# Eigenvector products at other places in TensorE's order, and a plain third weight for the last two groups of layer 0

## The chip, the cores and the metric

The kernel runs on one core of a Trainium2 chip. The metric is the time on the device in microseconds (us), from the start of the program to its end. Three runs of the kernel before took 2317.26, 2320.21 and 2320.10 us, so the median is 2320.1 us.

## What is computed

Four layers run one after the other over x of 128 x 64 x 256 values. Each adds what its branch gives to x and normalises the rows. Only layers 0 and 1 matter here:

```python
# layer 0: three graph convolutions, the adjacency multiplied twice (adj * S with S = adj)
h = relu(slconv(x, adj, adj, W1)); h = relu(slconv(h, adj, adj, W2)); slconv(h, adj, adj, W3)
x = layernorm(x + ...)
# layer 1: the eigenvectors of the normalised Laplacian of adj
L_norm = d_inv_sqrt[:, None] * (diag(deg) - A) * d_inv_sqrt[None, :]
_, U = eigh(L_norm)                       # 64 x 64
agg = einsum('mn,bnd->bmd', U.T, x); h = relu(agg @ W1 + b1)
x = layernorm(x + einsum('nm,bmd->bnd', U, h @ W2 + b2))
# layer 2: two graph convolutions and LSTMs over windows of 1 to 4 steps; layer 3: attention
```

U depends on `adj` alone. So it can be computed while layer 0 runs, and layer 1 is the first that needs it.

## The kernel before

The 8192 rows lie in 64 tiles of 128 rows, and four tiles make a group. **Layer 0** (function `layer0`, L1116) goes through 16 groups, the twelve groups 4 to 15 of the rows first and then 0 to 3 (`order`, L886). In this text a group is called by its place in that loop, so the last two are 14 and 15. **Layers 1 to 3** follow for all groups, in an order that a planner (`Plan`) writes out; the two phases share no work but a few row norms.

One group of layer 0 on TensorE is, in this order:

- the second weight (L1131): for each of two halves j, seven products of blocks instead of eight (`seven`, L1056), each of four calls of 128 x 256 columns. VectorE adds sums of blocks ahead of them (`sums_second`, L1109) and adds partial products together after them; ScalarE copies and applies relu. The result is `h2`, the 1024 features of 512 rows.
- after the first half, the adjacency product (`burst`) of the next group.
- the third weight (L1138): seven products again (`by_third`), each of eight calls of 128 columns. VectorE makes `sh[:, 0]`, `sh[:, 1]` and two differences in `h2` for them (L1141, L1142, L1147, L1148), each over 1024 elements per partition, and adds three results into `s3`. Between the second and the third of these products stand the four products of the next group's first weight (`weigh`).
- two more bursts of the next group, and `mix_rows`, which multiplies `s3` by the adjacency. VectorE then adds that into X.

In group 15 there is no next group, so `weigh` and the bursts are missing.

**The eigenvectors** (function `eigen`, L275) run beside this. They are a chain of small steps on VectorE: 62 Householder steps with one product on TensorE each (L415), two small products and two row broadcasts, six passes of bisection with 31 division steps each (L563), 63 further division steps (L603 to L608, tiles `tw` and `D`), and a tail with nine more products on TensorE (L643 to L749). The last of them fill `u2` and `ut2`, which layer 1 multiplies by.

The order of each engine's instructions is fixed when the program is built. `mm` in layer 0 (L963) emits a product and moves a reckoned clock `now` on by its expected time; `between` (L953) then lets `eigen` emit its next piece as soon as `now` has reached the time that `eigen` yielded. Its yields are `soon()` (L306), 0.45 us ahead of the end of VectorE's reckoned work, and `full()` (L309), which stands ahead of a product on TensorE. `free` is that reckoned end: each VectorE instruction of layer 0 and of `eigen` moves it on (class `Timed`, L42). So the place of an eigenvector product in TensorE's order, and of each eigenvector instruction between layer 0's instructions on VectorE, follow from these two clocks. After layer 0 whatever is left of `eigen` is emitted at once (L1169), and layers 1 to 3 come after it in every queue.

Of the kernel before, what the change touches and what calls it, by code (L numbers as in the profile page):

```python
# [11 lines left out]
F32 = mybir.dt.float32  # L12
# [262 lines left out]
def eigen(tc, stack, a, ident, cst, u2, ut2, now, free):  # L275
# [10 lines left out]
    until = [0.0]  # L286
    V, S, PE = Timed(nc.vector, free, until), nc.scalar, nc.tensor
# [5 lines left out]
    def sb(shape, tag):  # L293
        uid[0] += 1
        return wp.tile(shape, F32, tag=tag, name=f"{tag}_{uid[0]}")
# [10 lines left out]
        return max(free[0], until[0]) - 0.45  # L306

    def full(turns=0):
        return max(free[0], until[0]) + 0.3 + 0.6 * turns  # L309

    def mm(out, lhsT, rhs):
        PE.matmul(out, lhsT, rhs, start=True, stop=True)  # L312
# [37 lines left out]
    V.tensor_scalar(dm, C["eye"], y, None, op0=ALU.mult)  # L350
    pm = ps([N, N], "pa")
    yield full(4)
    mm(pm, m, dm)

# [27 lines left out]
    for i in range(N - 2):  # L382
# [3 lines left out]
        q = sb([N, 16], "q")  # L386
# [67 lines left out]
    d, e, ep, g = (de[:, j:j + 1] for j in range(4))  # L454
# [101 lines left out]
    lo2, h2, lam2 = lh[:, 0:1], lh[:, 1:2], lh[:, 2:3]  # L556
# [46 lines left out]
    for k in range(1, N):  # L603
        c = N - 1 - k
        t = sb([W, 1], "tw")
# [149 lines left out]
P = 128  # L755
# [13 lines left out]

RING = 4  # L770
QUADS = 1.17


def norm_parts(tc, pool, x, half, scalar=False):
# [54 lines left out]
def kernel(  # L829
# [26 lines left out]
    V, S, PE = nc.vector, nc.scalar, nc.tensor  # L856
# [5 lines left out]
    def tl(pool, shape, tag, **kw):  # L862
        uid[0] += 1
        return pool.tile(shape, F32, tag=tag, name=f"{tag}_{uid[0]}", **kw)
# [6 lines left out]
    wa = phase_a.enter_context(tc.tile_pool(name="wa", bufs=1))  # L871
# [4 lines left out]
    def load(pool, name, src, pattern, shape, **kw):  # L876
        t = pool.tile(shape, F32, name=name)
        nc.sync.dma_start(t, src.rearrange(pattern, **kw))
        return t
# [8 lines left out]
    def rows_of(g):  # L888

        return X[:, 4 * g:4 * g + 4, :] if g < RING else XA[:, 4 * (g - RING):4 * (g - RING) + 4, :]  # L890
# [16 lines left out]
    aw3 = load(wa, "aw3", a_w3, "(k p) f -> p k f", [P, 8, D], p=P)  # L907
# [45 lines left out]
    def between():  # L953
        while eig and eig[0] <= now[0]:
            try:
                eig[0] = next(eig[1])
            except StopIteration:
                eig.clear()
        if norms and due[0] <= now[0]:
            norms.pop(0)()  # L960
            due[0] = now[0] + 1.6

    def mm(out, lhsT, rhs, start=True, stop=True, **kw):  # L963
        PE.matmul(out, lhsT, rhs, start=start, stop=stop, **kw)  # L964
        now[0] += 2 * max(0.00084 * rhs.free_size(), 0.112)
        between()

    def run(out, pairs):
        for i, (lhsT, rhs) in enumerate(pairs):
            mm(out, lhsT, rhs, i == 0, i == len(pairs) - 1)  # L970

    def relu(dst, src):
        S.activation(dst, src, AF.Relu)  # L973

    def quads(c):
        for m in (slice(0, N), slice(N, P)):
            for h, hs in enumerate((slice(0, N), slice(N, P))):
# [3 lines left out]
    B11, B12, B21, B22 = (aw2[:, r:r + 2, c:c + 512] for r in (0, 2) for c in (0, 512))  # L981
    tw = wa.tile([P, 3, 2, 512], F32, name="tw")
    D11, D12, D21, D22 = (aw3[:, r:r + 4, c:c + P] for r in (0, 4) for c in (0, P))
    tv = wa.tile([P, 3, 4, P], F32, name="tv")
    m1 = pa.tile([P, 2, 512], F32, name="m1")
    h1 = pa.tile([P, 4, 512], F32, name="h1")
    m2 = pa.tile([P, 4, 512], F32, name="m2")
# [1 line left out]
    h2 = pa.tile([P, 8, 512], F32, name="h2")  # L989
    sh = pa.tile([P, 2, 4, 256], F32, name="sh")  # L990
    s3 = pa.tile([P, 4, D], F32, name="s3")
    A11, A12, A21, A22 = (m2[:, k:k + 2, r:r + 256] for r in (0, 256) for k in (0, 2))
    H11, H12, H21, H22 = (h2[:, c:c + 4, r:r + 256] for r in (0, 256) for c in (0, 4))
# [1 line left out]

    second = ((None, B11, B21, B22, tw[:, 2], B12, tw[:, 1], tw[:, 0]),
              (None, A11, A12, ss[:, 2], A22, ss[:, 0], ss[:, 1], A21))
    third = ((None, D11, D21, D22, tv[:, 2], D12, tv[:, 1], tv[:, 0]),
             (None, H11, H12, H12, H22, sh[:, 0], sh[:, 1], H21))
    free = [0.0]  # L1000
    VL = Timed(V, free, now)
# [3 lines left out]
    def step(then=None):  # L1005

        while pending:
            pending.pop(0)()
        if then:
            pending.append(then)  # L1010
        if norms:
            norms.pop(0)()

    def bank(tag="ps"):
        return tl(psa, [P, 512], tag, bufs={"ps": 4, "ch": 2, "b5": 1}[tag])

    def sums_of_weights(w, b12):
        VL.tensor_sub(w[7], w[3], b12)
        VL.tensor_sub(w[5], b12, w[1])
        VL.tensor_sub(w[6], w[3], w[5])  # L1020
        VL.tensor_sub(w[4], w[2], w[6])

    def burst(dst, src, c):
        to = dst.rearrange("p c (t h n) -> p h c t n", h=2, n=N)
        p = [bank().rearrange("p (c t n) -> p c t n", c=2, t=4) for _ in range(2)]
        for t in range(4):
            for k in range(2):
                for m, f, h, hs in quads(c + k):
                    PE.matmul(p[h][m, k, t, :], src[hs, t, f], sqT2[hs, hs], start=True, stop=True)  # L1029
        now[0] += QUADS  # L1030
        between()

        def result():
            for h in range(2):
                S.copy(to[:, h, c:c + 2], p[h])  # L1035

        step(result)
# [6 lines left out]
    def by_second(j):  # L1044

        def product(out, i, new):
            w, a = (x[i] for x in second)
            chained(out, [[(w[:, k, c * P:(c + 1) * P], a[:, k, :]) for k in range(2)] for c in (2 * j, 2 * j + 1)], new)

        return product  # L1050
# [5 lines left out]
    def seven(n, product, c11, c12, c21, c22, last):  # L1056

        def view(b):
            return b[:, :2 * n].rearrange("p (i n) -> p i n", i=2)

        def add(dst, b):
            VL.tensor_add(dst, dst, b)
            if last is relu:
                relu(dst, dst)

        ch = view(bank("ch"))
        product(ch, 1, True)
        step(lambda: S.copy(c11, ch))
        yield
        b2 = view(bank())  # L1070
        product(b2, 2, True)
        step(lambda: add(c11, b2))
        yield
        product(ch, 6, False)
        step(lambda: S.copy(c12, ch))
        yield
        b5 = view(bank("b5"))
        product(b5, 5, True)
        step(lambda: S.copy(c22, b5))
        yield  # L1080
        product(ch, 7, False)
        step(lambda: add(c22, ch))
        yield
        product(b5, 3, False)
        step(lambda: add(c12, b5))
        yield
        product(ch, 4, False)
        step(lambda: last(c21, ch))
        yield

    def weigh(t):
        p = bank()
        run(p, [(m1[:, k, t * P:(t + 1) * P], aw1[:, k, :]) for k in range(2)])
        step(lambda: relu(h1[:, t, :], p))
# [14 lines left out]
    def sums_second():  # L1109
        S1, S2, S4 = (ss[:, i] for i in range(3))  # L1110
        VL.tensor_add(S1, A21, A22)
        VL.tensor_sub(S2, S1, A11)
        VL.tensor_sub(A21, A11, A21)
        VL.tensor_sub(S4, A12, S2)

    def layer0():  # L1116
        n = NT // 4
        burst(m1, rows_of(order[0]), 0)
        step()
        for t in range(4):  # L1120
            weigh(t)
        step()
        sums_of_weights(second[0], B12)
        for c in (0, 2):
            burst(m2, h1, c)
        step()
        for g in range(n):
            sums_second()
            for j in range(2):
                q = [h2[:, 4 * c + 2 * j:4 * c + 2 * j + 2, r:r + 256] for r in (0, 256) for c in (0, 1)]  # L1130
                for _ in seven(256, by_second(j), *q, relu):  # L1131
                    pass
                if j == 0 and g + 1 < n:
                    burst(m1, rows_of(order[g + 1]), 0)
                if j == g == 0:
                    sums_of_weights(third[0], D12)
            q = [s3[:, r:r + 2, c:c + P] for r in (0, 2) for c in (0, P)]
            w3 = seven(P, by_third, *q, S.copy)  # L1138
            next(w3)
            next(w3)  # L1140
            VL.tensor_add(sh[:, 0], H21, H22)  # L1141
            VL.tensor_sub(sh[:, 1], sh[:, 0], H11)  # L1142
            for t in range(4):
                if g + 1 < n:
                    weigh(t)
                if t == 0:
                    VL.tensor_sub(H21, H11, H21)  # L1147
                    VL.tensor_sub(H12, H12, sh[:, 1])  # L1148
            for _ in range(4):
                next(w3)  # L1150
            if g + 1 < n:
                burst(m2, h1, 0)
            next(w3)
            if g + 1 < n:
                burst(m2, h1, 2)
            for t in (0, 2):
                mix_rows(g, t)
        step()
# [71 lines left out]
    V, S, G, Q = (Noted(plan, e) for e in ("DVE", "ACT", "POOL", "SP"))  # L1230
# [62 lines left out]
    def mixed(src, rhs):  # L1293
# [4 lines left out]
        plan.note("PE", [("matmul", (ps[h][m, c, t, :], src[hs, t, f], rhs[hs, hs]), {"start": True, "stop": True})  # L1298
                         for t in range(4) for c in range(2) for m, f, h, hs in quads(c)], QUADS)
        V.tensor_copy(to[:, 0], ps[0])  # L1300
# [433 lines left out]
```

## Time and profile before

One execution was profiled: 2317.55 us, of which the profiled span is 2315.7 us. Its mean granted TensorE clock is 0.988 of full speed.

| Stretch of the span | What runs | TensorE busy | VectorE busy |
|---|---|---|---|
| 55 to 105 us | layer 0 with Householder steps | 50.00 of 50 us | 41.39 us |
| 554 to 826 us | layer 0 with bisection and the further steps | 267.38 of 272 us | 231.87 us |
| 826 to 846 us | the tail of `eigen` alone | 3.89 of 20 us | 15.93 us |
| 846 to 2316 us | layers 1 to 3 | 1432.51 of 1470 us | 1069.36 us |

In this and the other views busy time is that of instructions that run; what stands in brackets behind a line of a timeline is how long the engine sat idle before it, and what ended that. TensorE appears in two rows: PE is the products and PEld is their weight loads. One product call of 32-bit numbers appears as two records. DVE is VectorE, ACT is ScalarE.

### The profile page before, as it was taken

The page shows a single profiled execution, that of the slowest core. Times are in us where ns is not written, and L with a number is a line of the kernel's source. Part 1 is how long each engine was busy: PE and PEld are TensorE (multiplying, and loading weights), DVE is VectorE, ACT ScalarE, POOL GpSimd, SP SyncE. Part 2 cuts the span into 40 slices and gives each one's busy share as a digit, 9 for nine tenths or more (in the row PEclk, how much of TensorE's full clock was granted, in tenths as well). Part 3 has the DMA queues.
Part 4 walks back from the last instruction along what each step waited for, and adds up shares of the span by engine and source line. Part 5 has one row for each costly group of instructions (what it writes and reads, how often), then busy time and mean ns, then how long its engine had stood idle before and what let it go on. Part 6 is the DMA issues. An engine that isn't in the chain of part 4 may idle for free.

```text
span 2315.7 us, 51333 instructions
## 1 busy us (share of the span) xinstructions
PE 2247.0 (97%) x20228; PEld 1988.2 (86%) x20228; DVE 1744.2 (75%) x5718; ACT 1200.2 (52%) x2896; POOL 137.8 (6%) x315
## 2 busy tenths in 40 slices
PE   8999999999999969999999999999999999999996
PEld 6788888878888858999999999899899899998895
DVE  5887877777888978665957967867867776868764
ACT  3444444443444425665656655555655655655654
POOL 0000000000000010000100100100000010000001
PEclk9999999999999989999999999999999999999998
DMA  7000000000000031000201221211211220312300
GB/s 241 11 10 11 10 11 12 18 10 10 11 10 1 13 124 43 20 1 19 87 27 47 76 65 40 76 67 47 76 56 49 67 74 23 112 58 92 99 19 19
DMA packets 80114, 107.88 MB, mean 47 GB/s; under 512 B 23296, under 2 KB 64256, under 8 KB 79872
## 3 DMA queue, kind: packets, MB, share of 16 engines
q1 hardware_dynamic: 79520, 104.32, 14.1%
q8 instruction: 159, 2.61, 0.5%
q14 instruction: 83, 0.68, 0.1%
q10 hardware_dynamic: 352, 0.28, 0.0%
HBM read 57.64 MB, written 45.09 MB: 44 GB/s over the span
## 4 chain that ended last, share of the span: by engine, by line
PE 87%; DVE 8%; issue 1%; ACT 1%; DMA 1%; POOL 1%; SPq 0%; ACTq 0%; DVEq 0%; POOLq 0%
PE ps L162 55%; PE ch L964 13%; PE ps L964 9%; PE b L964 7%; PE ps L1029 2%; DVE X L162 1%; DVE w L162 1%; PE pa L312 1%; POOL rs L162 1%; DVE st L162 1%; DVE D L52 1%; DVE gates L162 1%; DVE tw L52 1%; ACT gates L162 1%; DVE w L52 0%
## 5 line engine op out<-in xcount | busy, mean ns | idle before, releaser
L162 PE MATMUL ps<-w,wih 128*128 128x128 f32 (+2 forms) x2944 | 572.9, 298 | 5.5 <-DVE gates L162 4.9
L162 PEld LDWEIGHTS ps<-w,wih 128*128 128x128 f32 x2944 | 454.5, 191 | 39.8 <-issue 13.5
L162 PE MATMUL ps<-w,sums 128*128 128x128 f32 (+2 forms) x3104 | 476.9, 294 | 5.8 <-DVE w L162 5.2
L162 PEld LDWEIGHTS ps<-w,sums 128*128 128x128 f32 x3104 | 419.8, 191 | 23.4 <-DVE w L162 6.6
L162 ACT ACTIVATE gates<-gates,cbi 128x256 f32<-128x256 f32 (+4 forms) x736 | 315.7, 482 | 189.1 <-DVE gates L162 186.3
L162 DVE TENSOR_TENSOR gates<-gates,ps 128x512 f32<-128x512 f32 (+4 forms) x408 | 236.7, 585 | 190.3 <-PE ps L162 182.0
L162 ACT COPY gates<-ps 128x512 f32<-128x512 f32 (+4 forms) x408 | 205.7, 509 | 238.7 <-PE ps L162 233.4
L162 PE MATMUL ps<-hs,whh 128*128 128x128 f32 (+1 forms) x896 | 182.2, 285 | 2.3 <-DVE hs L162 2.3
L162 PE MATMUL ps<-w,whh 128*128 128x128 f32 (+1 forms) x896 | 181.1, 284 | 0.0
L162 PEld LDWEIGHTS ps<-hs,whh 128*128 128x128 f32 x896 | 140.6, 193 | 2.5 <-DVE hs L162 2.5
L162 ACT ACTIVATE gates<-ps,cbi 128x128 f32<-128x128 f32 (+2 forms) x368 | 119.8, 387 | 41.8 <-PE ps L162 39.3
L162 PEld LDWEIGHTS ps<-w,whh 128*128 128x128 f32 x896 | 139.7, 191 | 0.0
L973 ACT ACTIVATE h<-h 128x512 f32<-128x512 f32 x96 | 60.6, 632 | 138.1 <-DVE h L52 138.1
L964 PE MATMUL ch<-m,tw 128*128 128x256 f32 x512 | 121.9, 381 | 3.6 <-DVE h L52 3.5
L964 PE MATMUL b<-ss,aw 128*128 128x256 f32 x512 | 122.9, 379 | 0.0
L964 PE MATMUL ps<-aw,m 128*128 128x512 f32 x256 | 115.2, 601 | 1.5 <-DMA aw<-in_a_w_dram 1.5
L964 PEld LDWEIGHTS ch<-m,tw 128*128 128x128 f32 x512 | 96.4, 190 | 19.4 <-DVE h L52 6.0
L964 PEld LDWEIGHTS b<-ss,aw 128*128 128x128 f32 x512 | 96.4, 190 | 12.6
L162 POOL TENSOR_SCALAR rs<-mv 128x2 f32<-128x2 f32 x96 | 26.1, 280 | 1352.1 <-DVE mv L162 1350.8
L964 PEld LDWEIGHTS ps<-aw,m 128*128 128x128 f32 x256 | 47.7, 193 | 54.8 <-issue 52.2
L1035 ACT COPY m<-ps 128x512 f32<-128x512 f32 x96 | 51.4, 588 | 76.3 <-PE ps L1029 75.9
L162 PE MATMUL ps<-hs,sums 128*128 128x128 f32 (+1 forms) x448 | 90.6, 284 | 0.0
(359 smaller groups left out, 4101.6 us busy)
## 6 DMA issues: line engine op xcount, KB each, us to landing
far<-w SPq DMA_DIRECT2D x42, 512.0 KB, 2.8
w<-far SPq DMA_DIRECT2D x168, 128.0 KB, 3.2
X<-rest SPq DMA_DIRECT2D x24, 512.0 KB, 3.6
out_dram<-X SPq DMA_DIRECT2D x64, 128.0 KB, 1.8
rest<-XA SPq DMA_DIRECT2D x12, 512.0 KB, 2.6
rest<-X SPq DMA_DIRECT2D x12, 512.0 KB, 2.7
XA<-in_x_dram SPq DMA_DIRECT2D x22, 256.0 KB, 6.7
aw<-in_a_w_dram SPq DMA_DIRECT2D x3, 1024.0 KB, 10.2
```

The source lines that it names most:

```text
L52: return getattr(self.engine, name)(out, *args, **kw)
L162: getattr(e, name)(*[real(x) for x in args], **{k: real(v) for k, v in kw.items()})
L312: PE.matmul(out, lhsT, rhs, start=True, stop=True)
L964: PE.matmul(out, lhsT, rhs, start=start, stop=stop, **kw)
L973: S.activation(dst, src, AF.Relu)
L1029: PE.matmul(p[h][m, k, t, :], src[hs, t, f], sqT2[hs, hs], start=True, stop=True)
L1035: S.copy(to[:, h, c:c + 2], p[h])
```

## The change

Two edits. First, `full()` gives a time that is 0.3 us earlier. Second, in the last two groups (`PLAIN = 2`) the third weight is multiplied plainly: for each of four row tiles, eight calls of 256 columns add up over the 1024 features. There, the four VectorE instructions that prepare blocks of `h2` and the three that add into `s3` are not emitted, and ScalarE copies `s3` out of two full banks. So that the weight itself stays as loaded, one of its sums of blocks now goes to a fourth block of `tv` and not over `D12` in place.

```diff
     def full(turns=0):
-        return max(free[0], until[0]) + 0.3 + 0.6 * turns
+        return max(free[0], until[0]) + 0.6 * turns
...
-    tv = wa.tile([P, 3, 4, P], F32, name="tv")
+    tv = wa.tile([P, 4, 4, P], F32, name="tv")
...
-    third = ((None, D11, D21, D22, tv[:, 2], D12, tv[:, 1], tv[:, 0]),
+    third = ((None, D11, D21, D22, tv[:, 2], tv[:, 3], tv[:, 1], tv[:, 0]),
...
+    def plain():
+        for t in (0, 2):
+            p = bank().rearrange("p (t f) -> p t f", t=2)
+            for i in range(2):
+                run(p[:, i, :], [(h2[:, c, (t + i) * P:(t + i + 1) * P], aw3[:, c, :]) for c in range(8)])
+                step((lambda p=p, t=t: S.copy(s3[:, t:t + 2, :], p)) if i else None)
+                yield
+        for _ in range(3):
+            yield
...
-            w3 = seven(P, by_third, *q, S.copy)
+            w3 = seven(P, by_third, *q, S.copy) if g < n - PLAIN else plain()
             next(w3)
             next(w3)
-            VL.tensor_add(sh[:, 0], H21, H22)
-            VL.tensor_sub(sh[:, 1], sh[:, 0], H11)
+            if g < n - PLAIN:
+                VL.tensor_add(sh[:, 0], H21, H22)
+                VL.tensor_sub(sh[:, 1], sh[:, 0], H11)
             for t in range(4):
                 if g + 1 < n:
                     weigh(t)
-                if t == 0:
+                if t == 0 and g < n - PLAIN:
                     VL.tensor_sub(H21, H11, H21)
                     VL.tensor_sub(H12, H12, sh[:, 1])
```

In the plain form the first two yields hold row tiles 0 and 1, and the two after `weigh` hold tiles 2 and 3. The order in which layers 1 to 3 are written out is the same in both kernels on every engine.

More of the change, by code (lines that the diff above doesn't have):

```diff
@@ L771 @@
 QUADS = 1.17
+PLAIN = 2
 def norm_parts(tc, pool, x, half, scalar=False):
```

## The prediction

> **What bounds the kernel now.** I read the page, then busy time by stretches, then the timelines of TensorE and VectorE around the end of layer 0, then the chain that ended last, in order of time.
>
> ```profile
> PE 2247.0 (97%) x20228; PEld 1988.2 (86%) x20228; DVE 1744.2 (75%) x5718; ACT 1200.2 (52%) x2896; POOL 137.8 (6%) x315
> ```
>
> ```profile
> 784.00:826.00 42.00, 39.11 (x229) 34.01 (x228) 35.36 (x126) 15.49 (x39) 3.09 (x8) 1.00 0.18 61
> 826.00:845.00 19.00, 2.89 (x19) 1.72 (x20) 15.24 (x85) 2.17 (x9) 1.20 (x3) 0.56 0.59 240
> 845.00:848.50 3.50, 3.50 (x130) 3.50 (x132) 2.31 (x7) 1.09 (x2) 0.00 (x0) 0.50 0.02 5
> ```
>
> The columns are stretch, length, busy PE, PEld, DVE, ACT, POOL, granted clock, DMA share and GB/s. TensorE is the bound by its average, but from 826 to 845 it works 2.89 us of 19, while VectorE works 15.24. That hole is the place to look at.
>
> ```profile
> 809.58 1.95 PE L964 MATMUL ch<-aw,h 128*128 128x128 f32 x16
> ...
> 815.17 2.02 PE L964 MATMUL ch<-tv,sh 128*128 128x128 f32 x16 [1.86 <-DVE sh L52]
> ...
> 825.99 0.24 PE L644 MATMUL pa<-ident,w 64*64 64x64 f32 x1
> ```
>
> ```profile
> 812.55 1.21 DVE L52 TENSOR_TENSOR sh<-h 128x1024 f32<-128x1024 f32 x1
> 813.80 1.22 DVE L52 TENSOR_TENSOR sh<-sh,h 128x1024 f32<-128x1024 f32 x1
> 814.94 1.22 DVE L52 TENSOR_TENSOR h<-h 128x1024 f32<-128x1024 f32 x1
> 816.07 1.22 DVE L52 TENSOR_TENSOR h<-h,sh 128x1024 f32<-128x1024 f32 x1
> ```
>
> ```profile
> 825.23 0.70 DVE X L52
> ...
> 837.08 0.48 PE pa L312 x2
> ...
> 839.87 0.46 PE pa L312 x2
> 840.35 0.24 DVE junk L52 x2
> ...
> 845.42 9.76 PE ps L162 x234
> ```
>
> Layer 0's products end at about 826. The eigenvectors' transpose (L644) and all after it stand behind them, and the chain runs through small VectorE steps (DVE w, bc, junk) until layer 1 can start at 845. So the end of phase one is set by the eigenvector chain on VectorE; in group 15 the four block sums (812.55 to 817.2) delay it directly. Up to 554 it is TensorE (50 of 50 us busy).
>
> [...]
>
> **Part 1: full() 0.3 us earlier.** There is one such place per Householder step, so 62 times 0.3 = 18.6 us could be thought the gain. The built orders of both kernels say otherwise. Weighing the products of layer 0 that stand ahead of each eigenvector product by their rows' times (0.433 us for a 256-column call: eight records in 1.73 us; 0.223 for 128 columns: sixteen in 1.785), the places move by 0 to 1.9 us, one in each group by 4.3, and this does not add up: from the seventh group on the pattern is the same in every group, six steps each, and the last Householder product is only 0.9 us earlier. TensorE is full there, so nothing is won. Does it stall? The left vector (tile LV) is ready 1.4 to 3.4 us ahead of its product in the steady groups. The step that moves by 4.3 had 1.9 us, but its vector now stands ahead of layer 0's add into X and four sums on VectorE (about 3.0 us), and its predecessor moves 1.5 earlier, so 2 to 3 us remain. I take nothing; bounds -1 and +3 us, since the first groups differ.
>
> Behind the last step four full() follow closely. Before, TensorE waited 1.64 us at 559.79 for an add of layer 0 queued behind the eigenvector steps. The product that these wait for now stands 0.87 us (two calls) further ahead of the waiting product: I take 0.8 us won. At the last add into h of group 14's second weight (758.62 before) this gives 757.8, and two more division steps (a pair of VectorE instructions, 0.556 us) lie behind the chain there.
>
> **Part 2: plain third weight, groups 14 and 15.** TensorE: 32 calls of 0.433 = 13.84 us in place of 56 of 0.223 = 12.5, so +1.34 us a group. VectorE: four sums (4.86 us from first to last) and three adds (0.35 to 0.42) go, about 6 us a group, and the wait of 1.86 us in group 15. These sums stood in the chain, so the gain is nearly the whole. ScalarE copies four times in place of eight (0.59 against 0.37 us) and waits for nothing new that others need soon. Group 14's two bursts now stand together, but their copies still have mix_rows (1.9 us) before the next product needs them.
>
> **The sum along the new order.** VectorE ends the add at 758.4. Three pairs (1.67), the last (0.5) and the close of the pass (3.9, as from 767.54 to 771.44) put the 63 further steps at 764.5, against 771.45. Then 41 pairs of 0.507 us stand ahead of the add into X: it starts at 785.3, where TensorE has its input at 783.4. TensorE starts group 15's second weight at 783.81 - 0.8 + 1.34 = 784.35. VectorE then has add 0.6, four sums 2.44, pair 0.5, add 0.6, two pairs 1.0, add 0.6, ten pairs 5.1, add 0.6: 796.8. TensorE wanted that last add at 794.7 (six products of 1.73), so it stalls 2.1 us where it stalled 0.33. Product and half end at 798.6. VectorE: two pairs, add, seven pairs to 802.0; nine small steps with an add (3.1) and the rest to the transposed vector 3.6: 808.7; the next add ends at 809.3. The seventh product starts then; the transpose (now ahead of its last call) follows at 810.65, the plain weight from 811.35 to 825.2. Its first six calls cover the add and relu that its seventh needs: these come behind the transpose (812.9, 813.6 against 813.9). The broadcast product of the eigenvalues stands behind the plain weight; its input needs only 9.1 us from 812.9. So it goes at 825.2 (837.08 before), the next vector is ready 2.65 later (827.85), two adds into X stand ahead of the next step (1.2: 829.05), one copy of 0.27 now follows that stood earlier: 829.3 in place of 840.35. That is 11.0 us. The rest of the tail and layers 1 to 3 keep their order and move with it. The weight loads that begin at 822.6 to 824.8 and land within 13.5 us (838) are first needed 11 us after layer 1's start.
>
> 2317.55 - 11.0 = 2306.5 us. The profiled execution lies 2.55 us under the median of 2320.1, whose runs spread from 2317.26; from the median it would be 2309.1. I say 2307.5.
>
> **Rivals.** Below, times allow for the same 1 us.
> A, more is won: the hole shrinks to 6 or 7 us, TensorE may not fall to half clock, and 126 small products at 845 take 2.3 us (64 took 1.16) in place of 3.71; and VectorE may lag less at 794.7. 11 + 1.4 + 2 = 14.4: 2304. For it: TensorE is busy until 827. Against: 829 to 832 stays nearly empty.
> B, half is won: VectorE's runs of eigenvector steps go further ahead of layer 0's adds than I count, and each add into h that TensorE waits for costs it. A lag of 5 us more gives 2312.5. For it: stalls of 0.33 and 0.70 us in group 15 already. Against: durations are those of the same instructions.
> C, slower: the earlier places make TensorE wait for the left vector in each of the 62 steps. From 11/62 = 0.18 us a step the gain is gone; at 0.35 us 21.7 - 11 = 10.7 are lost: 2329. For it: TensorE is full until 554, so each such wait is lost whole. Against: the slack of 1.4 us and more.
> D, nothing: something else holds layer 1's start, such as the weight loads. 2318. Against: VectorE reads the first of them at 857.
>
> **How the numbers follow.** Forecast 0.68, A 0.14, B 0.09, C 0.05, D 0.04. The forecast's own range is 2304.5 to 2310.5 (-1 and +3 of part 1, half of the stall of 2.1, the spread of runs). With A and B the range is 2303.5 to 2312.5; beyond are C, D and the ends of A and B, under 0.2. What a measurement can tell from no change is 0.2%, some 4.6 us. Faster: forecast, A and B, 0.91; same: D, 0.04; slower: C, 0.05.
>
> **What would show it.** The product at 559.79 waits about 0.8 us; LV never delays TensorE; the further steps start near 764; the add into X of group 14 starts about 2 us after its input; the four sums are gone in groups 14 and 15; layer 1 starts near 834 and ends 11 us earlier. Waits of TensorE on LV, or a hole as long as before, would prove me wrong.

## The result and the profile after

The changed kernel took 2306.17 us (median of four runs, 2303.54 to 2307.19), the kernel before 2318.92 us in the same session (2317.26 to 2320.21). The ratio is 0.9944 with a 95% interval of 0.9932 to 0.9957, so some 13 us were won; 2307.5 had been predicted. The profiled execution took 2305.56 us, with a span of 2303.8 us.

The page's line of busy time after, and the three stretches that correspond to those of the prediction, in the same columns:

```profile
PE 2250.2 (98%) x20132; PEld 1985.7 (86%) x20132; DVE 1730.2 (75%) x5704; ACT 1196.0 (52%) x2892; POOL 137.0 (6%) x315
```

```profile
784.00:826.00 42.00, 40.47 (x182) 33.61 (x181) 32.83 (x144) 14.95 (x37) 3.07 (x8) 1.00 0.14 44
826.00:833.00 7.00, 2.58 (x19) 1.35 (x21) 5.75 (x31) 2.11 (x8) 1.08 (x3) 0.82 0.96 388
833.00:836.50 3.50, 3.50 (x132) 3.50 (x132) 2.31 (x7) 1.08 (x2) 0.00 (x0) 0.50 1.03 413
```

TensorE works 3.2 us more over the whole span and VectorE 14 us less (2250.2 against 2247.0, 1730.2 against 1744.2). The hole before layer 1 has shrunk from 19 us to 7, and layer 1 still begins at half clock. TensorE's timeline up to the hole and past it, after (start, duration, engine, line):

```profile
557.95 1.35 PE L965 MATMUL ch<-m,tw 128*128 128x256 f32 x5 [0.58 <-DVE h L52]
...
792.35 1.99 PE L965 MATMUL ch<-m,tw 128*128 128x256 f32 x8 [1.33 <-ACT h L1076]
...
796.26 1.99 PE L965 MATMUL ch<-m,tw 128*128 128x256 f32 x8 [0.20 <-DVE h L52]
...
809.92 0.24 PE L644 MATMUL pa<-ident,w 64*64 64x64 f32 x1
...
824.54 0.33 PE L312 MATMUL pa<-eig_c,bc 64*64 64x64 f32 x2
...
833.01 3.71 PE L162 MATMUL ps<-u,X 64*64 64x64 f32 x126
```

VectorE's timeline, at three places of the same stretch:

```profile
785.00 0.68 DVE L52 TENSOR_TENSOR X<-ps,X 128x512 f32<-128x512 f32 x1
...
810.20 0.22 DVE L52 COPY Z<-pa 64x64 f32<-64x64 f32 x1 [1.83 <-PE pa L644]
...
824.90 0.28 DVE L52 TENSOR_SCALAR w<-pa,lh 64x64 f32<-64x64 f32 x1 [4.09 <-PE pa L312]
```

The wait of 1.86 us for the block sums is gone and the broadcast product runs at 824.54 in place of 837.08. What was not there before: VectorE now waits for TensorE in the tail (1.83 and 4.09 us), because the products it needs stand in their place behind layer 0's.

**Three marks in place of one time.** Executions of one order scatter by some us, so single times hide effects of this size. Three points that every trace here has were used to cut each profiled execution into parts: the burst of small products inside group 2 (142.05 before, 141.23 after), layer 1's first product (`ps<-u,X`; 844.96 and 832.85), and the first product on tile `att` in layer 3 (`ps<-w,att`, 405.92 and 406.18 us later). Layers 1 to 3 keep their order on TensorE in all kernels here.

| Kernel | burst to layer 1, us | layer 1 to `att`, us | sum against before | time against before, 95% interval |
|---|---|---|---|---|
| before | 702.91 | 405.92 | | |
| after | 691.62 | 406.18 | -11.0 | -0.56% (-0.68 to -0.43) |
| after, again | 691.58 | 406.83 | -10.4 | -0.45% (-0.57 to -0.32) |
| places alone | 701.19 | 406.72 | -0.9 | -0.16% (-0.24 to -0.08) |
| plain alone | 694.71 | 406.88 | -7.2 | -0.37% (-0.49 to -0.24) |
| one plain group | 695.13 | 406.88 | -6.8 | -0.38% (-0.50 to -0.25) |
| three plain | 689.83 | 402.76 | -16.2 | -0.68% (-0.81 to -0.56) |
| three, again | 689.88 | 402.75 | -16.2 | -0.58% (-0.71 to -0.46) |
| four plain | 693.65 | 407.92 | -7.3 | -0.43% (-0.55 to -0.31) |
| hole filled | 691.40 | 404.61 | -12.8 | -0.43% (-0.56 to -0.30) |
| places further ahead | 691.57 | 405.62 | -11.6 | -0.51% (-0.64 to -0.38) |
| norms held | 691.60 | 406.62 | -10.6 | -0.46% (-0.58 to -0.34) |
| tail led | 689.41 | 404.26 | -15.2 | -0.53% (-0.67 to -0.40) |
| five passes | 690.13 | 404.96 | -13.7 | -0.59% (-0.72 to -0.47) |

The first column repeats to 0.05 us (after twice, three plain twice); the second repeats to 0.01 us with three plain groups, but only to 0.65 us with the changed kernel. So a difference of the sums below some 0.7 us says nothing. In the kernels with the new places one Householder product stands just ahead of the first mark that stands just behind it in the old order (49 of them follow the mark in place of 50), which makes their first column some 0.2 us too small. Most of the scatter lies outside the marks: the burst itself comes at 141.2 to 144.0 us, and from `att` to the end it takes 1058.7 to 1064.8 us in these fourteen executions. The two profiled times of before and after lie 11.99 us apart (2317.55 and 2305.56); by the marks some 11 us of that belong to the change.

### The profile page after: what moved, and what is told of

It reads as the page before. It is cut to its first block, busy times and chain, and to the rows that moved or that the text cites. A ratio compares the mean times of both kernels' runs of the same rounds, so it can differ in the third digit from the quotient of the medians.

```text
span 2303.8 us, 51099 instructions
## 1 busy us (share of the span) xinstructions
PE 2250.2 (98%) x20132; PEld 1985.7 (86%) x20132; DVE 1730.2 (75%) x5704; ACT 1196.0 (52%) x2892; POOL 137.0 (6%) x315
## 4 chain that ended last, share of the span: by engine, by line
PE 86%; DVE 9%; ACT 1%; DMA 1%; issue 1%; POOL 1%; SPq 1%; DVEq 0%; ACTq 0%; POOLq 0%
PE ps L162 53%; PE ch L965 14%; PE ps L965 9%; PE b L965 6%; PE ps L1030 2%; DVE w L162 1%; DVE X L162 1%; DVE gates L162 1%; DVE st L162 1%; POOL rs L162 1%; DMA w<-far 1%; ACT gates L162 1%; PE pa L312 1%; SPq L162 1%; DVE D L52 1%
```

## The experiments

The times against before are of the same chip and session; the three sessions of the experiments had 2317.52, 2314.68 and 2315.26 us for the kernel before.

### The two edits apart

```diff
# places alone
-PLAIN = 2
+PLAIN = 0
# plain alone
-        return max(free[0], until[0]) + 0.6 * turns
+        return max(free[0], until[0]) + 0.3 + 0.6 * turns
```

> The earlier places alone; all 16 groups keep the seven products. Theory (the two plain groups carry nearly all of the gain, the places only the shorter wait near 558 us): 2316 to 2318 us, 1 to 2.5 us under before; layer 1 starts near 843, and the four block sums with their wait of about 1.9 us are back in group 15. Rival (the places carry the gain, 0.3 us at each of 62 steps): 2306 to 2309. Rival (the places do nothing or harm): 2318.5 to 2321.

> The two plain groups alone, with the old places. Theory (the parts add up): 2307.5 to 2309.5 us, 9.5 to 11 under before; TensorE waits about 1.6 us near 560 again, layer 1 starts near 834.5. Rival (the places carry the gain): 2317 to 2319. Rival (the parts fill the same hole, so either gives most): 2306 to 2307.

Places alone took 2312.52 us (ratio 0.9984, 0.9976 to 0.9992), plain alone 2308.25 (0.9963, 0.9951 to 0.9976). The first time lies between the expected ranges. By the marks the places give 1.7 us up to layer 1, and 0.9 up to `att`; what the profiled execution is faster beyond that lies behind `att`, where it had the shortest stretch of all fourteen (1058.7 us), with no edit there. This leaves an open end: over fourteen runs the interval is 0.08 to 0.24%, 1.9 to 5.6 us, and the 0.9 us of the marks lie below it. It is the only row of the table in which marks and times disagree, and no run here says why. TensorE's timeline of places alone shows the old hole:

```profile
825.64 0.24 PE L644 MATMUL pa<-ident,w 64*64 64x64 f32 x1
837.27 0.47 PE L312 MATMUL pa<-eig_c,bc 64*64 64x64 f32 x2 [10.12 <-DVE bc L52]
```

Plain alone brings 8.2 us up to layer 1. The parts make 9.9 together and 11.3 when both are in, so the places are worth more once the sums are gone: in plain alone the transpose comes 3.2 us later against the burst (814.52 - 142.59 = 671.93; after 809.92 - 141.23 = 668.69). That the places carry the gain is refuted. The theories held only in the main: in places alone the wait for the block sums was 0.84 us and not 1.9, and in plain alone layer 1 started at 837.30 and not at 834.5.

### The Householder places further ahead

```diff
         V.tensor_copy(L[:N, 0, :], v.to_broadcast([N, N]))
-        yield full()
+        yield full(-2.5)
```

> The changed kernel with the 62 Householder places a further 1.5 us earlier, all other places as they are. Theory (the slack of the left vector is 1.2 to 2.9 us in the steady groups and under 1 us in several early ones, TensorE is full there, and a wait is lost whole): waits of TensorE on the tile LV appear, about 0.5 to 0.8 us at some 20 steps, and the time is 2315 to 2325 us. Rival (the order adapts, since the steps that follow a late product are late themselves, and nothing is lost): 2304 to 2309.

It took 2303.66 us, 0.9949 (0.9936 to 0.9962): nothing lost. From 25 to 556 us TensorE waits for the left vector in two steps only, 0.4 us together. The view of the tile LV in this kernel ends so:

```profile
who waited for it (us, times):
  DVE junk L52: 28.1, 29
  PEld pa L312: 0.4, 2
```

VectorE waited 54.0 us for such products before, 41.4 after and 28.1 here: with the product earlier, the next vector is earlier too. From the burst in group 2 to the one in group 10 (545.78 before, 545.02 after), which spans nearly all of the steps that are left, it takes 403.73 us before, 403.79 after, 403.78 with the places alone and 403.72 here. So the places of the 62 steps are worth nothing from that first burst on, and my theory of the fixed slack was wrong.

### How many groups are plain

```diff
-PLAIN = 2
+PLAIN = 1
# and 3, and 4
```

> New places, only group 15 plain. Theory (each group takes about 6 us of sums and adds out of VectorE's queue for 1.34 us of TensorE; group 15 also loses the wait of 1.86): 2310 to 2312.5 us, layer 1 starts near 838. Rival (the last group carries all, as only its sums stand in front of the transpose): 2306 to 2308. Rival (group 15 carries nothing): 2315 to 2317.

> New places, groups 13, 14 and 15 plain. Theory (in the changed kernel TensorE's order comes last in the tail: the transpose is queued 2.1 us and the eigenvalues' product 4 us after their inputs, so more relief of VectorE buys little and 1.34 us of TensorE is paid): 2305 to 2308 us. Rival (VectorE's chain still sets the end, another 4 to 5 us is to be had): 2300 to 2303. Rival (the extra TensorE work is lost whole, nothing back): 2307.5 to 2309.

> New places, groups 12 to 15 plain. Theory (with three the hole before layer 1 is nearly closed and the clock full, so from there each further group costs its 1.34 us of TensorE): 2301 to 2303 us beside 2300.7 with three. Rival (VectorE's chain still sets the end, so relief goes on paying): 2296 to 2299.

One took 2307.25 us (0.9962, 0.9950 to 0.9975), three 2300.70 (0.9932, 0.9919 to 0.9944), four 2306.32 (0.9957, 0.9945 to 0.9969; one of its six runs 2299.22). Up to layer 1 the steps are, from none to four: -6.1, -3.5, -1.8, +3.8 us. The relief runs out. One group's time lies in the range of the rival that has the last group carry all; its marks lie in the theory's (6.8 us), and the second group moves layer 1 a further 3.5 us. Four lie above both ranges. For three this is not what my theory said, but it isn't the rival's reason either: only 1.8 of its 5.2 us over the changed kernel come from the chain. The rest is TensorE's clock. Three plain groups, TensorE's timeline and two stretches by granted clock:

```profile
832.96 0.27 PE L312 MATMUL pa<-ident,U 64*64 64x64 f32 x2 [1.42 <-DVE u L52]
...
833.09 2.07 PE L162 MATMUL ps<-u,X 64*64 64x64 f32 x126
...
852.66 3.69 PE L162 MATMUL ps<-cw,w 128*128 128x256 f32 x16 [1.76 <-ACT v L162]
```

```profile
833.10:836.60 3.50, 3.50 (x145) 3.43 (x144) 3.35 (x9) 2.53 (x7) 1.24 (x3) 1.00 1.02 421
853.98:856.98 3.00, 3.00 (x57) 2.44 (x59) 2.92 (x7) 0.63 (x1) 0.20 (x1) 1.00 0.56 168
```

The only idle time left ahead of layer 1 is 1.42 us. The 126 small products take 2.07 us in place of 3.71, and the sixteen records at 852.66 take 3.69 us where the changed kernel needs 5.38 for them (at 854.27); the next experiment shows that this second part, 1.7 us, was luck. With four groups TensorE's own work is last: layer 1 starts 8.9 us after the eigenvectors' last product, which began at 828.55, because the rest of the plain weight stands between; and 6 us on it waits for ScalarE, whose queue holds group 15's norm pieces there. Of the +3.8 us, some 1.7 are half clock by estimate, half of 3.41 us: inside layer 0, behind waits of 1.04 and 1.70 us for ScalarE's copies, TensorE runs at 0.50 for 3.41 us. That stretch, and TensorE from layer 1 on, with four plain groups:

```profile
799.59:803.00 3.41, 3.41 (x10) 2.70 (x9) 3.07 (x16) 0.81 (x3) 0.00 (x0) 0.50 0.00 0
```

```profile
837.48 2.10 PE L162 MATMUL ps<-u,X 64*64 64x64 f32 x128 [0.76 <-DVE rs_row L1187]
839.50 2.05 PE L162 MATMUL ps<-bw,w 128*128 128x128 f32 x16
843.56 0.67 PE L162 MATMUL ps<-bw,w 128*128 128x128 f32 x4 [2.01 <-ACT sums L809]
```

### The hole filled with products that nobody reads

```diff
+    def fill(k):
+        b = bank("b5")
+        for _ in range(k):
+            PE.matmul(b[:, :D], ident, cw0[:, 0, :], start=True, stop=True)
...
     yield full()
+    FILL[-1](1)
     pu = ps([N, N], "pa")
...
     yield full()
+    FILL[-1](5)
     pt = ps([N, N], "pa")
```

> The changed kernel with six extra 256-column products, read by nothing, in the hole of TensorE before layer 1 (one ahead of the eigenvectors' product, five ahead of their transpose). Theory (what three plain groups won over two came mostly from TensorE keeping its full clock into layer 1; the fall to half clock costs about 3.4 us): layer 1's first 126 small products take about 2.1 us in place of 3.71, and the time is 2302 to 2304 us. Rival (the earlier chain was what counted, the clock is worth nothing): 2306 to 2308, layer 1 starting no earlier and the later stages no shorter.

The 3.4 us in it equal what three plain groups are shorter by from layer 1 to `att` (402.76 against 406.18 us). The kernel took 2305.03 us, 0.9957 (0.9944 to 0.9970): against the changed kernel, which gave 0.9955 and 0.9944, no gain that the times can tell. In the trace the extra products avoid one loss to half clock of two, less than I had expected. TensorE in this kernel:

```profile
834.38 2.07 PE L162 MATMUL ps<-u,X 64*64 64x64 f32 x126
...
854.28 5.23 PE L162 MATMUL ps<-cw,w 128*128 128x256 f32 x16 [1.80 <-DVE w L162]
```

The first loss is avoided (2.07 us against 3.71, 1.6 us), but the second, 20 us on, is still there. It stands behind waits of 0.95 and 1.80 us; three plain groups have 0.95 and 1.76 there and kept the clock. So two pauses of this length bring half clock in one kernel and not in another: of the fourteen traces, only the two of three plain groups have the fast 3.69 us there.

What differs is where the changes of the granted clock lie. In each trace all of them lie on one grid with steps of 3.41 us; in the changed kernel those at 830.45, 837.28, 854.34 and 857.76 us are 2, 5 and 1 steps apart. The grid lies differently in every execution: in the two of the changed kernel the clock falls ahead of layer 1 at 830.45 and at 832.25 us, although layer 1 starts at 832.85 and 833.28. Here are the steps of the grid around the two pauses, first in the changed kernel, then with three plain groups (no change of clock falls there, so the grid is carried over from those at 32.19 and 2257.68 us):

```profile
850.93:854.34 3.41, 1.41 (x65) 1.33 (x65) 3.41 (x14) 1.00 (x2) 1.10 (x4) 1.00 0.38 154
854.34:857.76 3.42, 3.42 (x9) 2.70 (x10) 2.14 (x6) 0.42 (x1) 1.44 (x2) 0.50 0.55 195
```

```profile
847.97:851.38 3.41, 1.98 (x108) 1.73 (x100) 3.41 (x12) 0.97 (x2) 1.41 (x3) 1.00 0.07 22
851.38:854.80 3.42, 2.14 (x10) 1.94 (x11) 3.34 (x12) 1.03 (x3) 2.41 (x4) 1.00 0.34 137
```

In the changed kernel one step holds both products and most of the idle time, 1.41 us of work, and the next step is at half clock. With three plain groups a boundary of the grid cuts the pauses in two, and each part keeps 2 us of work. So it is in all traces: in the twelve that lost the clock here the step before held 1.34 to 1.66 us of products, in the two that kept it no step held less than 1.98. Ahead of layer 1 in the kernel before, too, the step in front of the fall held 1.60 us (825.05 to 828.46).

In these traces, then, the second loss goes with where the grid happens to lie, and three plain groups were lucky in both profiled executions: 1.7 of their 5.2 us are not owed to the kernel. The first loss is different. Their hole of 1.42 us leaves 1.99 us of work in any step that holds all of it (3.41 less 1.42, an estimate), more than in any of the steps above that were followed by half clock. So 1.8 us of chain and 1.6 us of clock are left, 3.4 together; the times of the kernels side by side, further down, give 3.1.

### The wait that had a name

```diff
-        if norms:
+        if norms and not held[0]:
             norms.pop(0)()
...
+                held[0] = g == n - 1 and j == 0
                 for _ in seven(256, by_second(j), *q, relu):
```

> The changed kernel with the pieces of group 14's norm kept out of ScalarE's queue during the first seven products of group 15, so that the copy for which TensorE waited 1.33 us at 792.35 is in time. Theory (VectorE's late add two products further on sets the pace, the named wait is not the one that counts): the wait on ScalarE is gone, the wait on VectorE's add there grows from 0.20 to about 1.5 us, and the time stays at 2305.5 to 2307.5 us. Rival (the wait was real and its 1.33 us come back): 2304 to 2305.2.

2304.05 us, 0.9954 (0.9942 to 0.9966). As a time this lies in the rival's range, but against before it is the changed kernel's ratio (0.9944 and 0.9955). TensorE, the same two products:

```profile
792.45 1.99 PE L965 MATMUL ch<-m,tw 128*128 128x256 f32 x8 [1.02 <-ACT h L1077]
...
796.86 1.35 PE L965 MATMUL ch<-m,tw 128*128 128x256 f32 x5 [0.69 <-DVE h L52]
```

The named wait shrank only from 1.33 to 1.02 us, since the copy also stands behind a relu that waits for VectorE; but the next one grew from 0.20 to 0.69, and the second product starts 655.08 us after the burst here and 655.03 in the changed kernel. Layer 1 comes no earlier (691.60 and 691.58). What sets the pace is VectorE's late add; the wait on ScalarE in front of it was free.

### What is last in the tail now

```diff
# tail led: the transpose 0.9 us of reckoned time earlier, the two broadcast products 0.8 and 0.4,
# and VectorE's steps reckoned at 0.2 us from there on
-    yield full()
+    yield full() - 0.9
     pz = ps([N, N], "pa")
...
-    rn = co_[13]
+    rn, V.least = co_[13], 0.2
...
-        yield full()
+        yield full() - lead
         p = ps([N, n, N], tag)
# five passes
-PASSES = 6
+PASSES = 5
```

> The changed kernel with the transpose of the eigenvectors placed two calls earlier and the two broadcast products placed inside the plain weight of group 15 (after 24 and 28 of its 32 calls) in place of behind it. Theory (in the changed kernel TensorE's order comes last in the tail: the first broadcast product lies ready 4 us before its turn): layer 1 starts 2.5 to 3.5 us earlier against the bursts of layer 0, time 2 to 4 us under the changed kernel. Rival (VectorE's chain is as late anyway, or the products then wait and hold up the plain weight): within 1 us of it, or slower.

> The changed kernel with five of the six bisection passes (the eigenvalues are left coarser), so that VectorE's chain is about 20 us shorter. Theory (the chain sets layer 1's start, and with it out of the way TensorE has no hole at all): layer 1 starts 5 to 6 us earlier, at full clock, and the time is 6 to 9 us under the changed kernel. Rival (the weight loads or something else hold layer 1's start): at most 2 us under it.

> The changed kernel as it is, on the same chip as the next three, to have them beside it. Theory and rival alike: 0.5 to 0.65% under before; TensorE waits 2.4 us at the eigenvectors' transpose and layer 1's first 126 small products take 3.7 us.

> Groups 13, 14 and 15 plain, a second time, beside the changed kernel. Theory (the chain about 1.8 us earlier at layer 1's start, and no fall to half clock there, 1.6 us): 2.5 to 5 us under the changed kernel. Rival (the gain over the changed kernel was that of a lucky execution): within 1 us of it.

In one session the changed kernel took 2304.87 us (2303.99 to 2307.65), three plain groups 2301.77 (2301.12 to 2302.97), the led tail 2303.46 (2299.80 to 2304.69), five passes 2301.43 (2301.33 to 2302.78). Every run of three plain groups lies under every run of the changed kernel. TensorE with the led tail:

```profile
821.85 0.33 PE L312 MATMUL pa<-eig_c,bc 64*64 64x64 f32 x2
822.11 1.99 PE L965 MATMUL ps<-aw,h 128*128 128x256 f32 x8
824.50 0.29 PE L312 MATMUL pa<-eig_c,bc 64*64 64x64 f32 x2 [0.40 <-DVE bc L52]
```

Against the burst, the first broadcast product comes 3.5 us earlier (679.88 and 683.34) and layer 1 2.2 us earlier (689.41 and 691.58). Layer 1 starts at full clock, and from there to `att` it is another 2.6 us. So TensorE's order was last there, as the theory had it, if for less than the expected 2.5 to 3.5 us; in the times only 1.4 us show, within their scatter.

Five passes leave the eigenvalues coarser; the run shows only what a shorter chain would be worth. It leaves 20 us less of chain, and yet layer 1 comes only 1.45 us earlier, not 5 to 6, and the time is 3.4 us lower, not 6 to 9. TensorE with five passes:

```profile
807.39 1.99 PE L965 MATMUL ch<-m,tw 128*128 128x256 f32 x8 [0.73 <-ACT h L1076]
...
812.86 1.99 PE L965 MATMUL ch<-m,tw 128*128 128x256 f32 x8 [1.13 <-DVE h L52]
...
815.68 0.33 PE L312 MATMUL pa<-ident,U 64*64 64x64 f32 x4 [0.56 <-DVE u L52]
```

The tail's small products and its VectorE steps now lie among layer 0's work. What they cost in the hole for nothing they cost there in full: waits of 0.73, 1.13 and 0.56 us, and about 0.25 us for each of six products. Then TensorE has no hole ahead of layer 1, and the 690.13 us are its own work with these waits. So of the changed kernel's last hole about 1.5 us could be had by shortening the chain, 2.2 by the order of the tail, and 1.6 from the clock at the start of layer 1.

## Why the prediction was right

It was right in the time and in most of its steps, and part of the close agreement is luck.

- **The Householder phase wins nothing.** Right, to 0.1 us. Its reason was half right: TensorE is full, but the slack of 2 to 3 us that I counted for the left vector is no fixed store; with places 1.5 us earlier again TensorE waits 0.4 us in all.
- **The wait at 559.79 shrinks to 0.8 us.** It is 0.58 at 557.95.
- **Last add of group 14 at 757.8, further steps from 764.5, add into X at 785.3.** In the trace 757.63, 764.34 and 785.00, but that these agree is luck: the burst in group 2 comes 0.82 us earlier in this execution. Against the burst the last add comes only 0.2 us earlier than before (616.40 and 616.57), not 0.8, and the other two come 0.7 and 0.5 us later than predicted. What was won at 559.79 is mostly lost again in group 14, where TensorE now waits for ScalarE's copy, which the prediction did not have:

```profile
740.50 1.99 PE L965 MATMUL ch<-m,tw 128*128 128x256 f32 x8 [0.40 <-ACT h L1076]
```

- **TensorE stalls 2.1 us at 794.7 for VectorE's add.** It stalls 1.53, in two pieces, and the larger one has the name of another engine: ScalarE's copy was late. I had not foreseen that one; it cost nothing of its own, as the run with the norms held shows. The product behind the stall starts 0.3 us later than predicted, counted from the burst (655.03 for 654.75).
- **Transpose 810.65, broadcast product 825.2, layer 1 11.0 us earlier.** 809.92, 824.54, and by the marks 11.3 us. Against the burst, too, the first two fit to 0.2 us (668.69 for 668.60, 683.31 for 683.15).
- **Layers 1 to 3 move with it.** Up to `att` they take 0.26 us more. Layer 1 begins at half clock (0.50 from 833.00 to 836.50 us) as I took it in the forecast from the trace before (0.50 from 845.00 to 848.50); rival A, which had the clock kept, did not come about here. It came about with three and with four plain groups, with the led tail, with five passes and where the hole was filled (2.07 to 2.10 us for the small products, against 3.71).
- **Per group some 6 us of VectorE go, for 1.34 us of TensorE, and the gain is nearly the whole.** For group 15, plain first, 6.1 us came; for group 14 on top of it only 3.5, because by then TensorE was last in the tail. The sum of 11.0 was added up along the path and not by groups, and it came out although single steps were off by up to 0.7 us: the later ones made up for the earlier. (One figure is a slip: the four sums take 4.74 us from first to last; 4.86 is what their durations add up to.)
- **From the profiled execution to the median.** I allowed 1 us. By the marks such an allowance has no meaning: start and end of an execution scatter by 3 and 6 us with the same order. That the median came out 1.3 us from the forecast is inside that scatter and no proof of the allowance.

C and D are refuted: TensorE did not wait for the left vector, and no weight load held layer 1, although the loads now overlap its start (DMA share 1.03 at 833 us): no wait of TensorE from 826 to 860 us was ended by a load.

## What to carry to other kernels

Where two engines share the end of a stage, relief for one pays until the other is last: the third unit was worth 1.8 us where the first was worth 6.1, and the fourth lost 3.8, some 1.7 of them to the clock. So try the neighbouring values of such a constant; three was better than the two that were chosen (2301.77 and 2304.87 us side by side). Before you mend a wait, ask which late instruction stands right behind it; and compare effects of a few us between marks inside the trace, not between whole times, and see whether the clock fell at the same places in both traces.

## What the runs showed of the hardware

- In all fourteen traces the granted clock changes on a grid of 3.41 us, which lies differently in every execution (the fall ahead of layer 1 at 830.45 and at 832.25 us in two of the same kernel).
- Idle times of 0.95 and 1.8 us, close together, cost a further 1.5 to 1.7 us through the half clock after them where one step of that grid held 1.34 to 1.66 us of products (twelve traces, 16 records in 5.17 to 5.38 us), and nothing where no step held less than 1.98 (the two with three plain groups, 3.69 us). This is no general limit: in the changed kernel a step with 1.67 us of products (1639.40 to 1642.82) and one with 1.61 (2226.50 to 2229.91) kept the clock.
- In executions whose order is the same up to there (after, places alone, one, three and four plain groups) the burst in group 2 came at 141.2 to 144.0 us, and the stretch from `att` to the end took 1058.7 to 1064.8 us. What makes this scatter was not tried.
